# Tile 6 last in the last batch, and a recurrence that adds onto inputs kept in PSUM

## The chip, the cores and the metric

The kernel runs on one core of a Trainium2 chip. A core has five engines that run side by side, each in its own order: PE (matrix products, with a separate unit that loads weights, called PEld in the profile), ACT (functions such as exp, tanh and sigmoid), DVE (vector arithmetic), POOL (vector arithmetic too, slower) and SP, which here only issues DMA transfers. PE writes to PSUM, a small memory of banks from which ACT and DVE read; everything else is in SBUF or, outside the core, in DRAM. The metric is the device time of one execution in microseconds (us). Everything is in fp32, and a product of two fp32 operands counts as two matmul instructions in the profile, a transpose as one.

## The reference

The input x has 8 batches of 64 x 16 positions (1024 tokens) with 128 channels. Layer 0 is a convolution-like attention with 8 heads, two nested softmaxes and a feed-forward part. Layer 1, with which the change has to do, is this, token by token:

```
t = tokens(x)                                        # 8 x 1024 x 128
Bn = ln_t(t)                                         # LayerNorm without weights
Wi = Bn @ W.T
scores[b,i,j] = sum_d v[d] * tanh(Wi[b,i,d] + Wi[b,j,d])
t = t + softmax(scores, axis=-1) @ Bn                # attention
Wx = ln_t(t) @ Wf.T
Wx = (Wx - mean) * rsqrt(var + 1e-5) * gamma + beta  # mean and var over all 8192 tokens
y[b,-1] = 0;  y[b,n] = sigmoid(Wx[b,n] + y[b,n-1] @ V.T)     # 1024 steps
out = t + y
```

The scores are symmetric in i and j, so only the blocks on and above the diagonal need the tanh. The mean and the variance are taken over all tokens, so no step of the recurrence can begin before the last batch's attention is done.

## The kernel before

Both layers run batch by batch, layer 0 of batch b+1 beside layer 1 of batch b. Their instructions are not written in order: each piece of work is added to a planner (`Plan`) with the engine or engines that may do it, an estimated cost, the keys that it reads and writes, and a due time. `plan.emit()` then lists them for all engines, always taking the piece that can start first by the estimates and, among those, the one that is due first. So a change to what is added can move other instructions. What follows `plan.emit()` (line 1509) is written out in order.

**Attention of one batch in layer 1** (`layer1`, line 1275). The 1024 tokens are eight tiles of 128 rows. Row tile `it` computes the score blocks `it` to 7 of its rows. A group of rows is added up on DVE, POOL or ACT (lines 1164, 1168 and 1174), put through tanh on ACT (L1222; where ACT added, addition and tanh are one instruction, L1164), and multiplied with v on PE into the PSUM tile `sa` (L1242). When a row tile's scores are all there, ACT writes their exponentials to `E` (L1338); POOL halves the diagonal block and DVE adds its transpose (L1344, L1348). In most batches two row tiles share a pass; in the first and the last batch the order is a list of its own, `((4,), (5, 7), (6,), (0,), (1,), (2,), (3,))`.

As soon as row tiles 0 to `it` are done, `attention` (line 1357) handles output rows `it`: it transposes the blocks of `E` to the right of the diagonal into `ET` (L855, L867), multiplies the eight blocks with `Bn` (`attend`, L1371, with a 129th column that gives the softmax's denominator), and `add_to_x` divides and adds to `X` (L1375, L1376). After tiles 3 and 7 the four tiles are stored to `parked`, normalised (`layer_norm`: statistics on DVE, L814 and L815; the power -0.5 on POOL, L818 and L819; L824), transposed (`bT`) and projected (`projected`, L1265). `keep_wx` takes the statistics of the projection for the batch-wide mean (L1400) and copies it (L1401), in the last batch straight to `wx`.

**The recurrence** (from line 1512). The statistics of all batches are put together (L1514 to L1521) to a scale and an offset per channel. The 1024 steps of each batch are cut into 32 chunks of 32 steps that run side by side; each chunk starts 16 steps early from nothing (`EARLY`), so there are 16 + 32 = 48 steps, on 8 x 32 = 256 columns, in two halves of four batches. The inputs of 32 steps are scaled by DVE to `ws` (L1540). A step of a half is:

```
nc.tensor.matmul(to, ident, ws[:, l, bs, 0 : NCH - skip], start=True, stop=k == 0)   # L1552
nc.tensor.matmul(to, vf_sb, prev[half][:, :, skip:], start=False, stop=True)         # L1554
nc.scalar.activation(y[:, :, skip:], to, AF.Sigmoid)                                 # L1556
nc.vector.tensor_copy(ys[:, bs, l % NT, :, l // NT], y)                              # L1561, not in the first 16
```

The identity matmul brings the input into PSUM, the second adds the last state times V. When all steps are done, the output follows: 16 tiles of 512 columns, each of four transposes (L1570), an addition of the parked `X`, loaded as `xr` (L1526), on DVE (L1572), and a DMA by turns on ACT's queue and SP's (L1574).

Of the kernel before, what the change touches and what calls it, by code (L numbers as in the profile page):

```python
# [9 lines left out]
F32 = mybir.dt.float32  # L10
AF = mybir.ActivationFunctionType
ALU = mybir.AluOpType
AX = mybir.AxisListType
PSUM = bass.MemoryType.PSUM

P = 128
# [617 lines left out]
def fast_path(ctx: ExitStack, tc: tile.TileContext, a: dict, fits):  # L634
# [25 lines left out]
    def tile_of(pool, name, shape):  # L660
        return pool.tile(shape, F32, tag=name, name=name)
# [139 lines left out]

    stats = ring("stat", 7, [P, 4, 9])

    def layer_norm(src, kr, dst, kw, k, pri, on="POOL", then=None):


        st = stats[k]
        ks = ("stat", k)
        bn, mv, rs = st[:, :, 0:6], st[:, :, 6:8], st[:, :, 8]
        kw = kw if isinstance(kw, list) else [kw]  # L810

        def statistics(_):
            for j in range(4):
                nc.vector.bn_stats(out=bn[:, j, :], in_=src()[:, j, :])  # L814
                nc.vector.bn_aggr(out=mv[:, j, :], in_=bn[:, j, :])  # L815

        def power(_):
            nc.gpsimd.tensor_tensor(rs, mv[:, :, 1], eps, ALU.add)  # L818
            nc.gpsimd.tensor_tensor(rs, rs, neg_half[:, :4], ALU.pow)  # L819

        def normalise(e):
            if e == "DVE":
                for j in range(4):
                    nc.vector.tensor_scalar(  # L824
                        dst[:, j, :], src()[:, j, :], mv[:, j, 0:1], rs[:, j : j + 1], ALU.subtract, ALU.mult
                    )
            else:
                shape = [P, 4, C]
                nc.gpsimd.tensor_tensor(dst, src(), mv[:, :, 0:1].to_broadcast(shape), ALU.subtract)
                nc.gpsimd.tensor_tensor(dst, dst, rs.unsqueeze(2).to_broadcast(shape), ALU.mult)  # L830

        add(("DVE", 1.9), statistics, r=[kr], w=[ks], pri=pri)
        add(("POOL", 1.5), power, r=[ks], w=[ks], pri=pri)
        add((on, 1.1 if on == "DVE" else 2.2), normalise, r=[kr, ks], w=kw, pri=pri, give=then)

# [439 lines left out]
    def layer1(b):  # L1275
# [21 lines left out]

        E_at = E_first
        fills = [("fill", False), ("fill", True)]
        order = ((4,), (5, 7), (6,), (0,), (1,), (2,), (3,)) if early else shared  # L1300
        done, attended = set(), set()
        past = 0
        for pair in order:
# [48 lines left out]
            for it in range(NT):  # L1352
                if it not in attended and done.issuperset(range(it + 1)):
                    attended.add(it)
                    attention(b, it, X, kX, B, kB, E_at, L1)

    def attention(b, it, X, kX, B, kB, E_at, L1):

        for j0 in range(it + 1, NT, 4):
            js = range(j0, min(j0 + 4, NT))  # L1360
            through_bank(
                transposes([E_sb[:, E_at[it] + j - it, :] for j in js]), 0.08 + 0.12 * len(js),
                [("E", it, j) for j in js],
                copy(ET[:, j0 - 1 : j0 - 1 + len(js), :]), ("DVE", 0.15 + 0.132 * len(js)), [],
                [("ET", j) for j in js], L1,
            )

        def attend(bank):
            for j in range(NT):
                lhsT = E_sb[:, E_at[j] + it - j, :] if j <= it else ET[:, j - 1, :]  # L1370
                nc.tensor.matmul(bank[:, : C + 1], lhsT, B[:, j, :], start=j == 0, stop=j == NT - 1)  # L1371

        def add_to_x(_, bank):
            den = stats[5][:, 0, 0:1]
            nc.vector.reciprocal(den, bank[:, C : C + 1])  # L1375
            nc.vector.scalar_tensor_tensor(X[:, it, :], bank[:, :C], den, X[:, it, :], ALU.mult, ALU.add)  # L1376

        kg = kX + (it // 4,)
        through_bank(
            attend, 2.0,  # L1380
            [("E", j, it) for j in range(it + 1)] + [("ET", j) for j in range(it + 1, NT)]
            + [kB + (qh,) for qh in range(2)],
            add_to_x, ("DVE", 0.55), [kg], [kg], L1,
        )
        if it % 4 != 3:
            return
        qh = it // 4
        Xg = X[:, 4 * qh : 4 * qh + 4, :]
        add(
            ("SP", 4.0), lambda _: nc.sync.dma_start(  # L1390
                out=parked[b][512 * qh : 512 * qh + 512, :].rearrange("(t p) c -> p t c", p=P), in_=Xg
            ),
            r=[kg], w=[("parked", b, qh)], pri=L1,
        )
        layer_norm(lambda: Xg, kg, B2, kB2, 4, L1, "DVE" if b == NB - 1 else "POOL")

        kept = wx[:, b, 512 * qh : 512 * qh + 512] if b == NB - 1 else bT

        def keep_wx(_, bank):
            nc.vector.bn_stats(out=wx_stats[:, b, qh, :], in_=bank)  # L1400
            nc.vector.tensor_copy(kept, bank)  # L1401

        kq = ("e", 1, 1) if b == NB - 1 else ("bT",)
        projected(B2, kB2, wf_sb, (keep_wx, ("DVE", 1.4)), kq, L1, bT, ("bT",))
        if b < NB - 1:
            add(
                ("SP", 4.0),
                lambda _: nc.sync.dma_start(out=parked_wx[b][:, 512 * qh : 512 * qh + 512], in_=bT),
                r=[kq], w=[("wx", b, qh)], pri=L1,
            )  # L1410
# [95 lines left out]
    fetch_wx()  # L1506
    with tc.manual_schedule():
        plan.emit()
    main.close()


    rn = ctx.enter_context(tc.tile_pool(name="rn", bufs=1))
    mv = rn.tile([P, 2], F32, tag="mvb", name="mvb")
    nc.vector.bn_aggr(out=mv, in_=wx_stats.rearrange("p b s k -> p (b s k)"))  # L1514
    sc = rn.tile([P, 1], F32, tag="scb", name="scb")
    nc.vector.tensor_scalar(sc, mv[:, 1:2], EPS, None, ALU.add)
    nc.gpsimd.tensor_tensor(sc, sc, neg_half[:, 0:1], ALU.pow)
    nc.vector.tensor_tensor(sc, sc, gamma_sb, ALU.mult)
    off = rn.tile([P, 1], F32, tag="offb", name="offb")
    nc.vector.tensor_tensor(off, mv[:, 0:1], sc, ALU.mult)  # L1520
    nc.vector.tensor_tensor(off, beta_sb, off, ALU.subtract)  # L1521


    xr = rn.tile([P, NB, NT, C], F32, tag="xr", name="xr")
    for b in range(NB):
        nc.sync.dma_start(out=xr[:, b], in_=parked[b].rearrange("(p t) c -> p t c", t=NT))  # L1526

    EARLY = 16
    HB = NB // 2
    ws = rn.tile([P, LCH, NB, NCH], F32, tag="ws", name="ws")
    ys = rn.tile([P, NB, NT, NCH, LCH // NT], F32, tag="ys", name="ys")
    steps = wx.rearrange("p b (c l) -> p l b c", l=LCH)
    order = [LCH - EARLY + k for k in range(EARLY)] + list(range(LCH))
    for l in order[:LCH]:
        nc.vector.tensor_scalar(ws[:, l], steps[:, l], sc, off, ALU.mult, ALU.add)  # L1540
    with tc.tile_pool(name="ps_w", bufs=2, space=PSUM) as ps_w, tc.tile_pool(
        name="ps_t", bufs=4, space=PSUM
    ) as ps_t:
        prev = [None, None]
        for k, l in enumerate(order):
            early = k < EARLY
            skip = 1 if early else 0
            for half in range(2):
                bs = slice(half * HB, (half + 1) * HB)
                acc = ps_w.tile([P, HB, NCH], F32, tag=f"acc{half}", name=f"acc{half}")  # L1550
                to = acc[:, :, skip:]
                nc.tensor.matmul(to, ident, ws[:, l, bs, 0 : NCH - skip], start=True, stop=k == 0)  # L1552
                if k:
                    nc.tensor.matmul(to, vf_sb, prev[half][:, :, skip:], start=False, stop=True)  # L1554
                y = rn.tile([P, HB, NCH], F32, tag=f"y{half}", name=f"y{half}", bufs=3)
                nc.scalar.activation(y[:, :, skip:], to, AF.Sigmoid)  # L1556
                if k == EARLY - 1:

                    nc.vector.memset(y[:, :, 0:1], 0.0)
                if not early:  # L1560
                    nc.vector.tensor_copy(ys[:, bs, l % NT, :, l // NT], y)  # L1561
                prev[half] = y

        n = 0
        for b in range(NB):
            for g in range(2):
                pt = ps_t.tile([P, 4, C], F32, tag="yt", name="yt")
                for i in range(4):
                    t = 4 * g + i
                    nc.tensor.transpose(pt[:, i, :], ys[:, b, t].rearrange("p c j -> p (c j)"), ident)  # L1570
                ot = rn.tile([P, 4, C], F32, tag="ot", name="ot", bufs=4)
                nc.vector.tensor_tensor(ot, pt, xr[:, b, 4 * g : 4 * g + 4, :], ALU.add)  # L1572
                eng = nc.sync if n % 2 else nc.scalar
                eng.dma_start(  # L1574
                    out=a["out"][b].rearrange("(p t) c -> p t c", t=NT)[:, 4 * g : 4 * g + 4, :], in_=ot
                )
                n += 1


# [65 lines left out]
```

## Time and profile before

| | us |
|---|---|
| median of three runs | 5300.66 |
| their lowest and highest | 5299.17, 5303.35 |
| the profiled execution | 5300.69 |
| its span, first to last instruction | 5298.8 |
| ACT busy in the span | 4957.7 (94%) |
| PE busy | 4915.6 (93%) |
| DVE busy | 4739.3 (89%) |
| POOL busy | 4437.4 (84%) |

All lines of the profile are of that one execution. Times count from the span's start. A line of the timeline gives start, duration, engine, source line, operation, what is written and read with partitions x elements, the number of instructions put together, and in brackets how long the engine had been idle before and what released it. The granted clock is TensorE's, as a share of full speed; its mean over the span was 0.987.

The last batch's tanh work ends at 5206, the recurrence's first sigmoid starts at 5237.42 and its last at 5280.39, and the span ends at 5298.8.

### The profile page before, as it was taken

How to read it: one execution, taken by the hardware profiler on the slowest of the kernel's cores; microseconds unless marked ns; L12 is line 12 of the kernel's file. 1: busy time of each engine (PE TensorE's matmuls, PEld its weight loads, DVE VectorE, ACT ScalarE, POOL GpSimd, SP SyncE). 2: the span in 40 equal slices, each digit the busy share in tenths (PEclk: the TensorE clock that was granted, in tenths of full speed). 3: DMA queues.
4: the chain of work that ended last, by engine and by line, in shares of the span. 5: the costliest groups of instructions: out<-in, count | busy, mean ns of one | idle time of the engine just before them, and what ended most of it. 6: DMA issues, size and time to landing. Idle time of an engine off the chain costs nothing.

```text
span 5298.8 us, 184474 instructions
## 1 busy us (share of the span) xinstructions
PE 4915.6 (93%) x82181; PEld 3021.0 (57%) x82181; DVE 4739.3 (89%) x9090; ACT 4957.7 (94%) x3692; POOL 4437.4 (84%) x3064
## 2 busy tenths in 40 slices
PE   8899999999999999999999999999998999986567
PEld 6666656656665566556655566555664556552125
DVE  5788988889999999989998999989998999999886
ACT  4389999999999999999999999999999999999995
POOL 2366988679999899979999899989998989897992
PEclk9999999999999999999999999999999999998999
DMA  2000000000000000000000000000000000000001
GB/s 64 2 3 7 3 2 6 2 10 3 2 6 8 4 3 6 4 8 2 3 6 6 6 3 2 6 8 4 3 3 2 10 2 2 2 29 9 1 1 69
DMA packets 27669, 43.16 MB, mean 8 GB/s; under 512 B 2512, under 2 KB 19280, under 8 KB 26864
## 3 DMA queue, kind: packets, MB, share of 16 engines
q1 hardware_dynamic: 24832, 27.99, 1.6%
q8 instruction: 645, 10.57, 0.9%
q10 hardware_dynamic: 1872, 3.16, 0.2%
q14 instruction: 160, 1.31, 0.1%
q0 software_dynamic: 160, 0.13, 0.0%
HBM read 19.22 MB, written 12.06 MB: 6 GB/s over the span
## 4 chain that ended last, share of the span: by engine, by line
PE 67%; ACT 15%; DVE 11%; issue 5%; POOL 1%; DMA 0%; SPq 0%; ACTq 0%; DVEq 0%; POOLq 0%
PE sa L1242 23%; PE sc L948 14%; PE m L1050 13%; ACT th L1222 10%; DVE th L1168 3%; PE m L965 3%; ACT th L1164 3%; PE m L923 2%; PE m L982 2%; PE m L1371 2%; DVE stat_e L1027 2%; PE m L909 1%; DVE wx L990 1%; DVE th L1174 1%; PE m L1120 1%
## 5 line engine op out<-in xcount | busy, mean ns | idle before, releaser
L1174 POOL TENSOR_TENSOR th<-wiT 128x1024 f32<-128x1024 f32 (+55 forms) x2254 | 3255.7, 1479 | 308.9 <-PE sa L1242 270.3
L1222 ACT ACTIVATE th<-th 128x3210 f32<-128x3210 f32 (+57 forms) x1074 | 2926.5, 2767 | 27.0 <-DVE th L1174 15.6
L1242 PE MATMUL sa<-th,vpat 128*32 128x512 f32 (+33 forms) x24576 | 2045.9, 460 | 243.4 <-ACT th L1222 222.9
L1168 DVE TENSOR_SCALAR_CACHE_REDUCE th<-wiT 128x344 f32<-128x344 f32 (+61 forms) x2362 | 1945.8, 863 | 79.6 <-PE sa L1242 76.3
L1242 PEld LDWEIGHTS sa<-th,vpat 128*32 128x32 f32 x24576 | 715.7, 110 | 1186.2 <-issue 681.7
L1164 ACT ACTIVATE th<-wiT 128x501 f32<-128x501 f32 (+59 forms) x1544 | 1120.2, 797 | 16.1 <-PE sa L1242 14.9
L948 PE MATMUL sc<-xT,wx 128*32 128x256 f32 x16384 | 980.3, 380 | 2.2 <-issue 2.2
L1039 POOL TENSOR_TENSOR wx<-wx,stat_e 128x1024 f32<-128x1024 f32 x342 | 658.6, 1948 | 242.5 <-DVE stat_e L1030 153.9
L948 PEld LDWEIGHTS sc<-xT,wx 128*32 128x32 f32 x16384 | 549.9, 110 | 291.4 <-issue 45.5
L1050 PE MATMUL m<-wx 128*128 128x256 f32 x2400 | 563.1, 388 | 18.6 <-DVE stat_e L970 7.7
L1050 PEld LDWEIGHTS m<-wx 128*128 128x128 f32 x2400 | 449.6, 192 | 146.2 <-issue 45.6
L990 DVE TENSOR_TENSOR wx<-wx,m 128x1024 f32<-128x1024 f32 x330 | 396.9, 1206 | 38.6 <-PE m L982 36.8
L956 ACT ACTIVATE wx<-sc 128x1024 f32<-128x1024 f32 x342 | 340.3, 1022 | 93.8 <-PE sa L1050 35.9
L1042 DVE STREAM_TRANSPOSE wx<-wx 128x1024 f32<-128x1024 f32 x342 | 417.6, 1230 | 4.1 <-POOL wx L1039 3.6
L1039 POOL TENSOR_TENSOR e<-e,stat_e 128x1024 f32<-128x1024 f32 x170 | 327.1, 1946 | 97.6 <-DVE stat_e L1030 62.4
L1027 DVE TENSOR_REDUCE stat_e<-wx 128x128 f32<-128x2048 f32 x171 | 388.5, 2272 | 17.3 <-ACT wx L1024 16.1
L1024 ACT ACTIVATE wx<-wx 128x2048 f32<-128x2048 f32 x171 | 327.3, 1915 | 30.3 <-DVE wx L990 30.0
L982 PEld LDWEIGHTS m<-stat_e,ident 128*32 128x32 f32 x15808 | 224.0, 111 | 149.9 <-issue 76.7
L1050 PE MATMUL m<-e,wx 128*128 128x256 f32 x1184 | 278.6, 389 | 16.8 <-DVE e L1042 9.8
L1050 PEld LDWEIGHTS m<-e,wx 128*128 128x128 f32 x1184 | 221.7, 192 | 79.4 <-issue 21.7
L982 PE MATMUL m<-stat_e,ident 128*32 128x16 f32 x15808 | 229.2, 185 | 18.7 <-DVE stat_e L977 5.8
L1030 DVE RECIPROCAL stat_e<-stat_e 128x128 f32<-128x128 f32 x256 | 240.0, 938 | 0.2
(215 smaller groups left out, 4801.4 us busy)
## 6 DMA issues: line engine op xcount, KB each, us to landing
xT<-in_xt_dram SPq DMA_DIRECT2D x8, 512.0 KB, 3.4
th<-in_x_dram SPq DMA_DIRECT2D x8, 512.0 KB, 7.1
parked<-X SPq DMA_DIRECT2D x16, 256.0 KB, 2.3
xr<-parked SPq DMA_DIRECT2D x8, 512.0 KB, 6.9
parked_wx<-bT SPq DMA_DIRECT2D x14, 256.0 KB, 2.3
wx<-parked_wx SPq DMA_DIRECT2D x7, 512.0 KB, 3.7
out_dram<-ot ACTq DMA_DIRECT2D x8, 256.0 KB, 2.2
out_dram<-ot SPq DMA_DIRECT2D x8, 256.0 KB, 2.2
```

The costliest lines, as they stand in the source:

```text
L948: nc.tensor.matmul(sc[32 * a : 32 * a + 32, 256 * s : 256 * s + 256], u[:, rows], tokens[:, a], start=True, stop=True,)
L982: nc.tensor.matmul(bank[32 * a : 32 * a + 32, s * G : s * G + G], ident[:, 32 * s : 32 * s + 32], r1, start=True, stop=True,)
L990: nc.vector.tensor_tensor(quarters(e), quarters(e), r, ALU.mult)
L1027: nc.vector.tensor_reduce(r2, e2.rearrange("p q (m g) -> p q m g", g=G), AX.X, ALU.add)
L1039: nc.gpsimd.tensor_tensor(e3, e3, r2[:, q, :].unsqueeze(2).to_broadcast([P, M, G]), ALU.mult)
L1042: add(("DVE", 1.17), lambda _, e=e: nc.vector.transpose(e, e), r=[ke], w=[ke], pri=L0)
L1050: nc.tensor.matmul(bank()[:, :256], vp[:, t, :], keys[:, t], start=t == 0, stop=t == NT - 1)
L1164: nc.scalar.activation(rows(c)[:, r, :], wiT[:, i0 + begin[c] :], AF.Tanh, bias=w_i(c, r))
L1168: nc.vector.tensor_scalar(rows(c)[:, r, :], wiT[:, i0 + begin[c] :], w_i(c, r), 0.0, ALU.add, ALU.add, accum_out=next_unused())
L1174: eng.tensor_tensor(rows(c), wiT[:, i0 + begin[c] :].unsqueeze(1).to_broadcast(shape), w_i(c).unsqueeze(2).to_broadcast(shape), ALU.add,)
L1222: nc.scalar.activation(slot()[:, a:z], slot()[:, a:z], AF.Tanh)
L1242: nc.tensor.matmul(sa[32 * c : 32 * c + 32, s:s1], vpat[:, 31 - r0 - r : 63 - r0 - r], rows(c)[:, r, s - at0 - begin[c] : s1 - at0 - begin ...
```

## The change

1. In the last batch alone, row tile 6 moves from the third place of the order to the last one.
2. There, output rows 6 and 7 are not attended in one go: products that do not need tile 6's scores are summed ahead in a PSUM tile of their own (`scs[0]`, `scs[1]`), and the late ones (three) are added to them. The row tiles 4 to 7 take their LayerNorm statistics one by one.
3. The copy of the last half of `wx` is put behind the first three operations on the batch-wide statistics in the source, and a sigmoid of one column is written ahead of them.
4. The recurrence's inputs are no longer brought to PSUM by an identity matmul in each step. Four PSUM banks (two halves, four steps each, twofold) are written once by identity matmuls of 512 columns; after that DVE writes the scaled inputs of four steps and a half at a time straight into them, and V's matmul adds onto what is there (`start=False`). ACT writes its results directly to `ys` in the last 32 steps.
5. The output's layout on the chip has rows that belong to the first and the second half of each chunk's steps, and `xr` is loaded in 16 pieces of 256 KB instead of 8 of 512 KB. The 8 output tiles of the first half are made from step 32 of 48 on, two transposes a step, beside the remaining steps; the other 8 follow after the last step.

```
-        order = ((4,), (5, 7), (6,), (0,), (1,), (2,), (3,)) if early else shared
+        order = ((4,), (5, 7), (0,), (1,), (2,), (3,), (6,)) if b else ((4,), (5, 7), (6,), (0,), (1,), (2,), (3,))
+        order = order if early else shared
...
+        keys = {j: ("E", j, it) if j <= it else ("ET", j) for j in range(NT)}
+        ends = b == NB - 1 and it >= NT - 2
+        if ends:
+            at, kp = scs[it % 2][:, : C + 1], ("sc", it % 2)
+            late = [j for j in range(NT) if min(j, it) == NT - 2]
+            for js in ([j for j in range(NT) if j not in late], late):
+
+                def some(_, js=js):
+                    for j in js:
+                        lhsT = E_sb[:, E_at[j] + it - j, :] if j <= it else ET[:, j - 1, :]
+                        nc.tensor.matmul(at, lhsT, B[:, j, :], start=j == 0, stop=j == late[-1])
+
+                add(("PE", 0.22 * len(js)), some, r=[keys[j] for j in js] + [kB + (qh,) for qh in range(2)], w=[kp], pri=L1)
+            add(("DVE", 0.55), lambda _: add_to_x(_, at), r=[kp, kg], w=[kg], pri=L1)
...
+        if b == NB - 1 and it // 4 == 1:
+            bn, mv = stats[4][:, it % 4, 0:6], stats[4][:, it % 4, 6:8]
+
+            def statistics(_):
+                nc.vector.bn_stats(out=bn, in_=X[:, it, :])
+                nc.vector.bn_aggr(out=mv, in_=bn)
+
+            add(("DVE", 0.42), statistics, r=[kg], w=[("stat", 4)], pri=L1)
...
-            nc.vector.tensor_copy(kept, bank)
+            if b == NB - 1 and qh == 1:
+                last_half.append((kept, bank))
+            else:
+                nc.vector.tensor_copy(kept, bank)
...
+    nc.scalar.activation(off, eps[:, 0:1], AF.Sigmoid)
     nc.vector.bn_aggr(out=mv, in_=wx_stats.rearrange("p b s k -> p (b s k)"))
     nc.vector.tensor_scalar(sc, mv[:, 1:2], EPS, None, ALU.add)
     nc.gpsimd.tensor_tensor(sc, sc, neg_half[:, 0:1], ALU.pow)
+    for kept, bank in last_half:
+        nc.vector.tensor_copy(kept, bank)
...
+    for h in range(2):
+        for b in range(NB):
+            nc.sync.dma_start(out=xr[:, b, h].rearrange("p r k -> p (r k)"), in_=pieces(parked[b], h))
...
-    for l in order[:LCH]:
-        nc.vector.tensor_scalar(ws[:, l], steps[:, l], sc, off, ALU.mult, ALU.add)
...
+        ws = [[tile_of(ps_w, f"ws{half}{i}", [P, 4, HB, NCH]) for i in range(2)] for half in range(2)]
+        for i in range(2):
+            for half in range(2):
+                nc.tensor.matmul(
+                    ws[half][i].rearrange("p l b c -> p l (b c)"), ident, ident.unsqueeze(1).to_broadcast([P, 4, P]),
+                    start=True, stop=True,
+                )
+
+        def inputs(k):
+            skip = 1 if k < EARLY else 0
+            for l in (slice(0, 1), slice(1, 4)) if k == 0 else (slice(0, 4),):
+                for half in range(2):
+                    nc.vector.tensor_scalar(
+                        ws[half][k // 4 % 2][:, l, :, skip:],
+                        steps[:, order[k] + l.start : order[k] + l.stop, half * HB : half * HB + HB, 0 : NCH - skip],
+                        sc, off, ALU.mult, ALU.add,
+                    )
+
+        def tile_out(b, h):
+            pt = ps_t.tile([P, 4, C], F32, tag="yt", name="yt")
+            for r in range(4):
+                nc.tensor.transpose(pt[:, r, :], ys[:, b, h, r].rearrange("p i c -> p (i c)"), ident)
+                if r % 2:
+                    yield
+            ot = rn.tile([P, 4, C], F32, tag="ot", name="ot", bufs=4)
+            nc.vector.tensor_tensor(ot, pt, xr[:, b, h], ALU.add)
+            eng = nc.sync if b % 2 else nc.scalar
+            eng.dma_start(out=pieces(a["out"][b], h), in_=ot.rearrange("p r k -> p (r k)"))
...
-                nc.tensor.matmul(to, ident, ws[:, l, bs, 0 : NCH - skip], start=True, stop=k == 0)
+                to = ws[half][k // 4 % 2][:, k % 4, :, skip:]
                 if k:
-                    nc.tensor.matmul(to, vf_sb, prev[half][:, :, skip:], start=False, stop=True)
-                y = rn.tile([P, HB, NCH], F32, tag=f"y{half}", name=f"y{half}", bufs=3)
+                    nc.tensor.matmul(to, vf_sb, prev[half][:, :, skip:], start=False, stop=True, skip_group_check=True)
+                if early:
+                    y = rn.tile([P, HB, NCH], F32, tag=f"y{half}", name=f"y{half}", bufs=3)
+                else:
+                    y = ys[:, bs, l // HL, l % 4, l % HL // 4, :]
                 nc.scalar.activation(y[:, :, skip:], to, AF.Sigmoid)
...
-                if not early:
-                    nc.vector.tensor_copy(ys[:, bs, l % NT, :, l // NT], y)
...
+            if k % 4 == 3 and k + 5 < len(order):
+                inputs(k + 5)
+            if k >= EARLY + HL:
+                next(first_half, None)
+        for _ in first_half:
+            pass
+        for _ in outputs(1):
+            pass
```

## The prediction

> **What bounds the kernel now.** I read first a table of stretches (columns: us of the stretch, then PE, PEld, DVE, ACT, POOL busy us with counts, granted clock, DMA share, GB/s).
>
> ```profile
> 4600.00:4800.00 200.00, 180.12 (x2450) 99.51 (x2446) 183.37 (x487) 200.00 (x179) 182.75 (x135) 0.97 0.08 25
> 4880.00:5060.00 180.00, 105.22 (x972) 27.40 (x968) 147.97 (x280) 180.00 (x62) 167.47 (x106) 0.99 0.00 1
> 5210.00:5236.00 26.00, 15.80 (x100) 12.16 (x100) 15.14 (x52) 0.00 (x0) 2.99 (x5) 0.80 0.20 68
> 5240.00:5280.00 40.00, 40.00 (x361) 40.00 (x360) 26.30 (x84) 24.62 (x91) 0.00 (x0) 1.00 0.09 37
> 5280.00:5298.80 18.80, 9.17 (x68) 6.92 (x66) 10.94 (x19) 0.50 (x2) 0.00 (x0) 0.87 0.61 227
> ```
>
> ACT is busy without a gap until the last tanh; then it does nothing for 26 us, the close of the last batch. In 5240 to 5280, the recurrence, PE is busy all the time and ACT 24.6 of 40. The last 18.8 us are the output. So four stages, four limits: ACT; a serial chain; PE; DVE.
>
> The chain of work that ended last shows the close (start, us, what):
>
> ```profile
> 5206.25 1.13 PE sa L1242 x16
> 5207.40 0.71 ACT E L1338
> 5209.60 2.07 PE m L1371 x16
> 5212.30 2.07 PE m L1371 x16
> 5215.00 2.06 PE m L1371 x16
> 5219.43 3.59 PE m L1371 x32
> 5225.62 1.03 POOL stat L819
> 5229.10 2.09 PE m L1265 x2
> ```
>
> Tile 3's scores come last, and all row tiles from 3 on wait for them: five attends of 16 matmuls (L1371), statistics, two projections. Then lines of the timeline: the hinge, an early and a later step, and additions on DVE behind which ACT fell dry:
>
> ```profile
> 5231.22 0.70 DVE L1400 BATCH_NORM_STATS2 wx_stats<-m 128x6 f32<-128x512 f32 x1 [2.17 <-PE m L1265]
> 5231.83 0.67 DVE L1401 COPY wx<-m 128x512 f32<-128x512 f32 x1
> 5236.13 1.28 ACT L1556 ACT_TABLE_LOAD   x1 [28.03 <-DMA xr<-parked]
> 5238.58 0.27 ACT L1556 ACTIVATE y<-acc 128x124 f32<-128x124 f32 x1 [0.71 <-PE acc L1554]
> 5251.35 0.27 ACT L1556 ACTIVATE y<-acc 128x124 f32<-128x124 f32 x1 [0.17 <-PE acc L1554]
> 4842.91 17.87 DVE L1174 TENSOR_TENSOR th<-wiT 128x768 f32<-128x768 f32 x16 [0.38 <-PE sa L1242]
> 4860.81 2.10 ACT L1222 ACTIVATE th<-th 128x2280 f32<-128x2280 f32 x1 [2.19 <-DVE th L1174]
> 4512.94 10.81 DVE L1174 TENSOR_TENSOR th<-wiT 128x568 f32<-128x568 f32 x1
> ```
>
> Call S the start of the last statistics of wx, 5231.22.
>
> **The change part by part.** Sums go against the profiled run, 5300.69 (span 5298.8 and 1.9 around it), 0.03 over the median 5300.66.
>
> *Last batch, ACT's stretch (tile 6 moved from third to last).* Until about 4836 all queues issue what they issued. From there to the last tanh ACT does the same scores in other groups: summed at 0.833 ns an element plus 0.10 to 0.19 an instruction, 0.35 us less. The stall of 2.19 at 4860.81 stood behind additions before tile 6's scores, slowed to 17.87 us (10,656 elements; at 1.157 ns, by the 13.28 us for 11,472 at 4829.26, 12.3); the groups are cut anew, so I take it away. The last score matmuls are 32 of 128 columns instead of 16 of 388: 1.22 (the row at 4862.97) against 1.07. For new gaps I take 0.5, bounds 0 and 5: what the 7.2 us stall of the row at 4512 leaves at most of a lead that on DVE and POOL was 15 us at the end (their last additions end at 5192). Together -0.35 - 2.19 + 0.15 + 0.5 = -1.9 (-2.4 to +3).
>
> *The close.* Before, from the last score matmul's end (5207.32) to S: 23.9. After, the chain is: exponential 0.08 + 0.36 (128x256, at 4864.89), halving on POOL 0.08 + 0.46, transpose 0.33, addition on DVE 0.33, the late attend products 0.7 (of the sixteen of tiles 6 and 7 three come late, and thirteen are summed beforehand), twice reciprocal, X, statistics 1.85 (5223.04 to 5224.23 gives 0.54 for the first two and 0.4 for a pair of statistics), POOL 1.48, normalising to bT 1.68 (5226.68 to 5228.36), bT 0.74, projection with the clock still at 0.50 2.12. Sum 10.2, so -13.7 (bounds -12.5 and -15, the second with a warm projection: 1.12 at 5218.30). The attends of tiles 3 to 5 and the statistics and projection of tiles 0 to 3 now lie under ACT's stretch; what hides them there is that POOL was idle for 16.15 us before 5208.18 and PE busy 5.65 of the 10 us from 5200. Without that cover their 10.5 us (5208.85 to 5219.4) would come back.
>
> *Head of the recurrence.* The copy of wx, though deferred in the source, still stands between statistics and aggregate: no gain. New: four identity matmuls of 512 columns which prime PSUM banks, the first waiting for that copy (S+1.34). Cold each costs 2.08, warm 1.12, as L1265's. Writing of inputs waits for the first: S+3.47, where before the scale is ready too (5234.60 = S+3.38). Two pieces, then the table load 1.28, which the change means to move to the start: but in the issued order that sigmoid comes before the first exponential, and a load stays before the recurrence. First sigmoid S+5.8 (before S+6.20). Behind the four matmuls the first V matmul waits on PE: S+7.7 (S+9.7 if all stay cold). Before, the steady rhythm traced back from the last sigmoids (5279.94 less 46 steps) puts step 1's first sigmoid at S+7.64; after, S+7.7 + 0.47 = S+8.17. So +0.5 (0 to +2.5). The early sigmoid's extra table load at the start lies in the 1.30 us gap before the first exponential (30.60): 0, at most +1.3.
>
> *46 steps.* Before, a half step is 0.447 (5250.91 to 5251.35 to 5251.80), equal for 124 and 128 columns: four PE instructions, whose weight loads lie 0.112 apart. After, two of the four go, and the half's own chain is next: sigmoid 0.277, to PE 0.055, PE start to ACT start 0.47 (four transposes 5208.16 to the copy at 5208.85 is 0.69, less two of 0.112). 0.80 a step instead of 0.893: -4.3. Bounds 0.754 (weights ahead) and 0.893 (no gain): -6.4 to 0. The 64 copies of ys on DVE were beside PE: 0.
>
> *Half of the output beside the last steps.* New on PE: 32 transposes, by turns before a V matmul (0.112 to 0.22 each time); on ACT's queue four DMA issues of 0.34; each waits for an `ot` that DVE makes behind two writes of inputs (0.69 each), and the sigmoids behind it wait too. Two bunches of transposes at 0.5, four issues at 0.34 partly in ACT's 0.25 a step of idle, one wait of about 0.9: +2 (0.5 to 4).
>
> Recurrence: +0.5 - 4.3 + 2 = -1.8.
>
> *Output.* Eight of sixteen `ot` remain: 8 x 0.692 (2.60 to 2.69 for four, less waits as before) = -5.5, and of the 1.16 us in which they wait for DMAs some 0.2: -5.7 (-4.5 to -6.5). Loads of xr (16 of 256 KB, 4 MB in 12 us at some 400 GB/s) end well before the first `ot`: 0.
>
> **Sum:** -1.9 - 13.7 - 1.8 - 5.7 = -23.1: 5277.6.
>
> **The rivals.**
> 1. *The recurrence stays as long* (step 0.89: the path through ACT, PSUM and PE costs more than the transposes' row says). For it: the first cold step took 0.83 from V matmul to sigmoid. Then +4.3: 5282; with stalls at their upper bound 5284.
> 2. *The clock stays at 0.50* since PE is then busy only half the time. Rows: it rose 4.2 us after PE's return at 5235.3, with PE busy without gaps. Cold, PE start to ACT start is 0.83 (5237.75 to 5238.58), a step 1.16: 46 x 0.36 = +16.6, 5294.2: no change that can be measured (a measurement tells about 0.2%, 10.6 us). Against: 4880 to 5060 holds 0.99 with PE busy 105 of 180.
> [...]
> 3. *Slower:* tile 6's additions, last now, hold ACT up. DVE has 24 of them (20,188 elements, 23.4 us) ahead of ACT's last groups. One like 4512.94 costs 10.1 us over its 0.7, while POOL ran additions back to back. To end above 5311.3 ACT must lose 33 us on top of a lead of 15: five such hold-ups in the last tile. Four give 5277.6 + 40.4 - 15 = 5303, five 5313. Against: there was one of this size among the rows I read, and POOL was idle at this place.
>
> [...]
>
> **How the numbers follow.** Forecast 0.55, rival 1 0.25, rival 2 0.08, rival 3 0.05, and 0.07 for a loss in ACT's stretch or the close that I have not listed, half of it under the bound of 0.2%. Faster 0.87, same 0.08, slower 0.05. The bounds of the terms, taken as independent, give the forecast 5270 to 5286; with rival 1, and the edge of the unlisted, 5268 to 5289 leaves out about 0.2.
>
> **What the profile would show.** Right: some 17 us instead of 31.2 from the last tanh's end (5206.2) to the first sigmoid; S near 5215.6; a sigmoid every 0.40 us; 39 us from step 1's first sigmoid to the last, instead of 41.8; eight `ot` after it and 12.7 us to the end instead of 18.4. Wrong: PE's clock at 0.5 past S+12; ACT waiting for L1174 in the last 60 us; sigmoids that wait for a DMA issue; steps still 0.89 apart.

## The result: 0.3% slower

Over 16 runs each, the changed kernel has a median of 5317.26 us (5305.64 to 5323.26) and the kernel before 5300.26 (5290.00 to 5304.87). The ratio is 1.0034, with a 95% interval of 1.0027 to 1.0042: slower by some 18 us. The forecast was 5277.6, in a range of 5268 to 5289, with 0.05 on slower. It was wrong in its sign.

The profiled execution of the changed kernel took 5319.27 (span 5317.3), 18.6 more than that of the kernel before. Of this, 5.0 lie where both programs issue the same instructions in the same order: the first instruction of ACT that differs starts at 4835.11 before and at 4840.15 after. Why is not known; the last section shows how far that point lies apart between profiles. So from here on stages are counted from that instruction, in each profile, called the fork. S is, as in the prediction, the start of the last statistics of wx. All times in us; each entry is the difference of two starts or ends of the timeline.

| stage | before | predicted | after |
|---|---|---|---|
| fork to the end of the last tanh | 371.1 | 369.0 | 368.8 |
| to the end of the last score matmul | 1.1 | 1.3 | 4.2 |
| to S | 23.9 | 10.2 | 10.6 |
| S to the last sigmoid's end | 49.5 | 47.7 | 64.4 |
| to the end of the span | 18.1 | 12.4 | 29.1 |
| sum | 463.7 | 440.6 | 477.2 |

The close is as short as forecast. The loss is in the recurrence and the output. Three stretches from the table of stretches of the changed kernel (us, busy us of PE, PEld, DVE, ACT, POOL with counts, granted clock, DMA share, GB/s):

```profile
5228.00:5256.00 28.00, 24.04 (x124) 16.61 (x122) 19.11 (x21) 16.04 (x60) 0.00 (x0) 0.95 0.26 102
5256.00:5288.00 32.00, 18.29 (x111) 14.91 (x110) 12.17 (x15) 9.56 (x38) 0.00 (x0) 0.73 0.26 95
5290.00:5314.00 24.00, 1.56 (x11) 0.85 (x9) 4.15 (x6) 0.00 (x0) 0.00 (x0) 0.62 0.26 91
```

And the kernel before, while it loaded xr and while it stored the output:

```profile
5234.00:5242.00 8.00, 6.29 (x39) 6.04 (x39) 7.88 (x21) 3.67 (x11) 0.00 (x0) 0.66 0.99 393
5283.00:5296.00 13.00, 6.17 (x40) 3.96 (x38) 8.26 (x13) 0.00 (x0) 0.00 (x0) 0.93 0.84 310
```

In the changed kernel the DMA share is 0.26 in all three, at 91 to 102 GB/s: no engine is busy all the time, and the DMA engines are on average a quarter busy. Such an even quarter is what 4 of 16 engines working all the time would look like. Before, it was 0.99 and 393 GB/s during the loads and 0.84 and 310 GB/s during the output. The waits from S to the end (engine, line, waited for: us in total, times, longest):

```profile
DVE ot L1597 <- DMA out_dram<-ot: 25.2, 8, 7.4
ACT ys L1621 <- DVE ot L1597: 15.9, 3, 8.3
```

`ot` waits for one of its four buffers, whose transfer is not through; ACT's next sigmoid waits behind the DMA issue on its queue, which waits for `ot`. On the timeline:

```profile
5228.94 1.28 ACT L1621 ACT_TABLE_LOAD   x1 [15.32 <-DMA xr<-parked]
5231.89 0.27 ACT L1621 ACTIVATE y<-ws 128x124 f32<-128x124 f32 x1 [1.10 <-PE ws L1616]
5244.62 0.50 ACT L1621 ACTIVATE ys<-ws 128x128 f32<-128x128 f32 x2 [0.35 <-PE ws L1616]
5245.48 0.50 ACT L1621 ACTIVATE ys<-ws 128x128 f32<-128x128 f32 x2 [0.35 <-PE ws L1616]
5270.26 0.69 DVE L1597 TENSOR_TENSOR ot<-yt,xr 128x512 f32<-128x512 f32 x1 [5.33 <-DMA out_dram<-ot]
5270.98 0.55 ACTq L1599 DMA_DIRECT2D out_dram<-ot  x1
5271.57 0.45 ACT L1621 ACTIVATE ys<-ws 128x128 f32<-128x128 f32 x2 [6.47 <-DVE ot L1597]
5278.39 1.29 DVE L1597 TENSOR_TENSOR ot<-yt,xr 128x512 f32<-128x512 f32 x2 [7.44 <-DMA out_dram<-ot]
5280.30 0.45 ACT L1621 ACTIVATE ys<-ws 128x128 f32<-128x128 f32 x2 [8.28 <-DVE ot L1597]
5305.87 0.69 DVE L1597 TENSOR_TENSOR ot<-yt,xr 128x512 f32<-128x512 f32 x1 [3.69 <-DMA out_dram<-ot]
```

Steps run at 0.86 (5244.62 to 5245.48) until the output begins. Then ACT stands for 6.47 and 8.28: the issue at 5270.98 waits for the `ot` before it, and the sigmoid at 5271.57 for the issue. From 5269 to 5285 PE is busy 5.6 of 16 us; its granted clock is 0.50 there (1.00 from 5232 to 5268), and a step takes 1.16 (sigmoids at 5281.47 and 5282.63). After the last step five of the eight remaining `ot` wait for transfers again, 12.1 in all.

The chain of work that ended last shows the close, and what is new in it:

```profile
5208.32 1.79 PE m L1375 x16
5210.11 0.86 PE m L1266 x2
5210.97 2.25 PE sa L1243 x50
5213.24 0.39 ACT E L1340
5218.18 1.02 POOL stat L819
5221.66 2.09 PE m L1266 x2
5225.21 6.43 PE ws L1575 x8
```

The last score matmuls (L1243) stand on PE behind the attend of tile 5 and the projection of tiles 0 to 3; so 4.2 pass from the last tanh to their end, not 1.1.

### The profile page after: what moved, and what is told of

Its sections match the earlier page's. It is cut to its first block, busy times and chain, and to the rows that moved or that the text cites. A ratio compares the mean times of both kernels' runs of the same rounds, so it can differ in the third digit from the quotient of the medians.

```text
span 5317.3 us, 184017 instructions
## 1 busy us (share of the span) xinstructions
PE 4917.1 (92%) x81997; PEld 3010.9 (57%) x81997; DVE 4731.8 (89%) x9022; ACT 4957.7 (93%) x3691; POOL 4444.7 (84%) x3069
## 4 chain that ended last, share of the span: by engine, by line
PE 67%; ACT 15%; DVE 10%; issue 5%; POOL 1%; DMA 1%; ACTq 0%; SPq 0%; DVEq 0%; POOLq 0%
PE sa L1243 23%; PE sc L949 14%; PE m L1051 13%; ACT th L1223 10%; PE m L966 3%; DVE th L1169 3%; ACT th L1165 3%; PE m L924 2%; PE m L983 2%; PE m L1375 2%; DVE stat_e L1028 2%; PE m L910 2%; DVE wx L991 1%; PE m L1121 1%; PE m L856 1%
## 5 line engine op out<-in xcount | busy, mean ns | idle before, releaser
L1223 ACT ACTIVATE th<-th 128x3210 f32<-128x3210 f32 (+56 forms) x1075 | 2928.8, 2765 | 24.9 <-DVE th L1175 17.8
L1243 PE MATMUL sa<-th,vpat 128*32 128x512 f32 (+34 forms) x24576 | 2045.1, 460 | 233.8 <-ACT th L1223 212.0
L1243 PEld LDWEIGHTS sa<-th,vpat 128*32 128x32 f32 x24576 | 715.2, 110 | 1173.1 <-issue 682.2
L1025 ACT ACTIVATE wx<-wx 128x2048 f32<-128x2048 f32 x171 | 326.9, 1912 | 31.6 <-DVE wx L991 31.3
```

The costliest lines, as they stand in the source:

```text
L1223: nc.scalar.activation(slot()[:, a:z], slot()[:, a:z], AF.Tanh)
L1243: nc.tensor.matmul(sa[32 * c : 32 * c + 32, s:s1], vpat[:, 31 - r0 - r : 63 - r0 - r], rows(c)[:, r, s - at0 - begin[c] : s1 - at0 - begin ...
```

## The experiments

Theory A: loads of xr and stores of the output run on 4 of the 16 DMA engines, because their outermost dimension has four entries: the new layout reads and writes DRAM as 4 pieces x 32 chunks x 2 KB, the old one as 128 rows, of 4 KB in the loads and of 2 KB in the output. Theory B: DMA issues between the sigmoids and the sharing of queues are the cause. Each ratio is to the kernel before, run beside it on the same chip; its medians lie between 5291 and 5305 us on the five chips that were used, so a median is read against its own neighbour.

**Chunks outermost (e1).** The partitions are ordered chunk by piece instead of piece by chunk, and `ys` with them; so the sigmoids write with a step of four elements.

```
-        return tokens.rearrange("(c h i r) k -> h i c (r k)", h=2, i=4, r=4)[h]
+        return tokens.rearrange("(c h i r) k -> h c i (r k)", h=2, i=4, r=4)[h]
...
-    ys = rn.tile([P, NB, 2, 4, 4, NCH], F32, tag="ys", name="ys")
+    ys = rn.tile([P, NB, 2, 4, NCH, 4], F32, tag="ys", name="ys")
...
-                nc.tensor.transpose(pt[:, r, :], ys[:, b, h, r].rearrange("p i c -> p (i c)"), ident)
+                nc.tensor.transpose(pt[:, r, :], ys[:, b, h, r].rearrange("p c i -> p (c i)"), ident)
...
-                    y = ys[:, bs, l // HL, l % 4, l % HL // 4, :]
+                    y = ys[:, bs, l // HL, l % 4, :, l % HL // 4]
```

> The changed kernel with one thing different: in the transfers of xr and of the output the 32 chunks, not the 4 pieces of a chunk, are the outermost dimension on the DRAM side, and ys is laid out to match. Bytes, packet size (2 KB) and all waits stay. Theory A (a transfer whose outermost dimension has four entries is given to 4 of the 16 DMA engines: 102 GB/s and a DMA share of 0.25 in the changed kernel, where before had 400 GB/s): the share goes to near 1, xr lands within some 12 us, no ot waits over 1 us, ACT never waits for an ot over 2 us. Last sigmoid ends at S+50 (47 steps of 0.85 from S+8.1, and 2 of stalls), the end 13 later, S+63 instead of S+93.5: 31 us less than the changed kernel, about 5286. Theory B (DMA issues on ACT's queue between the sigmoids and the sharing of queues are the cause, whatever the layout): DMA share and time stay, 5312 to 5320.

Ratio to the kernel before 0.9989 (0.9980 to 0.9998), median 5294.90 against 5301.39. The loads, and a sigmoid in a late step:

```profile
5219.00:5229.00 10.00, 9.30 (x29) 4.88 (x28) 7.28 (x11) 4.32 (x13) 0.55 (x1) 0.75 0.96 337
5250.43 0.40 ACT L1621 ACTIVATE ys<-ws 128x128 f32<-128x128 f32 x1 [0.30 <-PE ws L1616]
```

The DMA share is 0.96, the table of waits from 5200 on has no `ot` that waits for a transfer, and last sigmoid to end is 13.1 instead of 29.1: theory A. The recurrence, 61.5, was expected at 50. The edit brought a cost of its own that I had not counted: with a step of four elements a sigmoid of 128 columns takes 0.40 instead of 0.28, and a step 1.19 (sigmoids at 5239.03 and 5240.22, at a clock of 1.00). From 5242 to 5258 the clock was 0.50 as well, and a step took 1.29 (5242.70 and 5243.99).

**Output left out of the step loop (e2).** The two lines `if k >= EARLY + HL: next(first_half, None)` are left out.

> The changed kernel, but no output tile is made beside the steps: all 16 follow after the last sigmoid; the layout of the transfers stays as in the changed kernel. Theory A (transfers at 102 GB/s are the limit from S on): xr takes 4.19 MB / 0.102 = 41 us from S+0.5, hidden by the steps; last sigmoid near S+48; then 16 output transfers of 2.57 us, 41 us: end near S+92, as in the changed kernel (S+93.5), so 5312 to 5319. Theory B (DMA issues between the sigmoids are the cause): the stalls go and the output takes 18.4 us as before: end near S+67, some 5291.

Ratio 1.0026 (1.0015 to 1.0037), median 5315.11. From S to the end 65.1 + 31.3. But the edit did not do what I meant: the framework that places instructions put eight `ot` between the steps all the same, with waits of up to 8.9 on ACT. So this is one more run of nearly the changed kernel, and it tells nothing between A and B.

**The layout alone in the kernel before (e3).**

```
-        nc.sync.dma_start(out=xr[:, b], in_=parked[b].rearrange("(p t) c -> p t c", t=NT))
+            nc.sync.dma_start(out=xr[:, b, h].rearrange("p r k -> p (r k)"), in_=pieces(parked[b], h))
...
-                    nc.vector.tensor_copy(ys[:, bs, l % NT, :, l // NT], y)
+                    nc.vector.tensor_copy(ys[:, bs, l // 16, l % 4, l % 16 // 4, :], y)
...
-                eng.dma_start(
-                    out=a["out"][b].rearrange("(p t) c -> p t c", t=NT)[:, 4 * g : 4 * g + 4, :], in_=ot
-                )
+                eng.dma_start(out=pieces(a["out"][b], g), in_=ot.rearrange("p r k -> p (r k)"))
```

> The kernel before, with only the changed kernel's layout of xr, ys and the output's transfers (16 loads, outermost dimension 4); recurrence, attention and the place of the output as before. Theory A: loads hidden behind the steps, but the 16 output transfers take 16 x 2.57 = 41 us and a landing after the first ot at 5281.5 instead of 17: about +25, 5325 (5318 to 5330). Theory B: no difference from before, 5298 to 5303.

Ratio 1.0068 (1.0052 to 1.0083), median 5331.69. Loads, then output:

```profile
5240.00:5265.00 25.00, 25.00 (x227) 25.00 (x226) 12.96 (x49) 15.46 (x57) 0.00 (x0) 1.00 0.27 102
5282.00:5324.00 42.00, 8.51 (x32) 5.86 (x32) 8.21 (x12) 0.00 (x0) 0.00 (x0) 0.54 0.26 99
```

Here no DMA is issued on ACT's queue between the sigmoids, and the recurrence takes 50.2 (49.5 before), but the output 49.6 instead of 18.1. The layout alone costs 31 us in the output, 6 more than expected: B can't explain that.

**Eight entries (e10).** The same kernel as e3 with partitions of 8 pieces of two steps x 16 chunks, so the rows are of 1 KB and there are twice as many transfers.

```
-        return tokens.rearrange("(c h i r) k -> h i c (r k)", h=2, i=4, r=4)[h]
+        return tokens.rearrange("(s c h i r) k -> s h i c (r k)", s=2, h=2, i=8, r=2)[s, h]
```

> The kernel before with a layout of xr and output whose outermost dimension has eight entries (8 x 16 rows of 1 KB, 128 KB a transfer, 32 loads and 32 output transfers) instead of four (e3) or 128. Theory A in the form: a transfer uses as many of the 16 DMA engines as its outermost dimension has entries: DMA share near 0.5 during the loads and, in the output, about twice the 102 GB/s of four entries, so 200 GB/s; 4.19 MB of output in 21 us, from the last sigmoid to the end 23 to 30 (18.1 before, 49.6 with four entries). If it is a threshold (anything under 16 goes to four engines): share 0.25, 49 us. If any outermost dimension over four is spread over all: share over 0.8, below 22 us.

One execution, 5313.64 against 5290.99 of the kernel before. Loads, then output:

```profile
5236.00:5250.00 14.00, 13.59 (x101) 13.30 (x101) 11.91 (x28) 7.71 (x28) 0.00 (x0) 0.82 0.53 185
5284.00:5308.00 24.00, 7.79 (x36) 5.62 (x34) 8.02 (x12) 0.00 (x0) 0.00 (x0) 0.60 0.53 170
```

Share 0.53; last sigmoid to end 30.8. So with 4, 8, 32 and 128 entries the share during the loads is 0.26, 0.53, 0.96 and 0.99. Of 16 engines, 4 and 8 at work all the time would be 0.25 and 0.5; with 32 and 128 entries nearly all were at work. The packets show it too: the trace has the start and the duration of each one. During the loads four packets of 2 KB are under way for 84% of the time in the changed kernel (5228 to 5256), seven to nine for over 85% in e10 (5236 to 5250), and 15 to 17, of 4 KB, for 85% in the kernel before (5234 to 5242). A packet of 2 KB has the same median of 84 ns in the changed kernel and in e1, so it is the number of engines at work that differs, and not their speed.

**The attention half of the change alone (e4).** All of the changed kernel up to the planner's end, with recurrence and output of the kernel before.

> Only the first half of the change: tile 6 last, attends of tiles 6 and 7 summed ahead, statistics one by one; recurrence and output as before. From the trace of the changed kernel: ACT's stretch -2.3, the last score matmuls on PE +3.1, from their end to S 10.6 instead of 23.9 (-13.3): together -12.5, 5288 (5284 to 5292). If the common part of the program, which is 5 us longer in the changed kernel's profile without a change in it, is longer because of something in this half, then 5293; if the order's gain is an artefact of the one profile, 5300.

Ratio 0.9977 (0.9968 to 0.9987), median 5288.35 against 5301.39. From the fork 452.4 instead of 463.7: 368.7, 4.2, 10.6, 50.5, 18.4. By the stages this half brings 11 us, by the medians 13, as expected; some 2 us of it are not the order's, as the account of the prediction below shows.

**Four transfers for each tile (e5).** The changed kernel's own `ys`, each tile moved in four pieces of 32 chunks.

```
-            nc.sync.dma_start(out=xr[:, b, h].rearrange("p r k -> p (r k)"), in_=pieces(parked[b], h))
+            for i in range(4):
+                nc.sync.dma_start(
+                    out=xr[32 * i : 32 * i + 32, b, h].rearrange("p r k -> p (r k)"), in_=pieces(parked[b], h)[i]
+                )
...
-            eng = nc.sync if b % 2 else nc.scalar
-            eng.dma_start(out=pieces(a["out"][b], h), in_=ot.rearrange("p r k -> p (r k)"))
+            eng = nc.sync if b % 2 or h == 0 else nc.scalar
+            for i in range(4):
+                eng.dma_start(
+                    out=pieces(a["out"][b], h)[i], in_=ot[32 * i : 32 * i + 32].rearrange("p r k -> p (r k)")
+                )
```

> The changed kernel with its own layout of ys (contiguous writes of the sigmoids), but each load of xr and each output tile is cut into four transfers of 64 KB, one for each of the 4 pieces, so that the outermost dimension has 32 entries; the first half's are all issued on SP's queue. Theory A (4 of 16 DMA engines): DMA share near 1 during the loads, no ot waits for a transfer over 2 us, steps of 0.85 without stalls over 1 us; from S the last sigmoid ends at +50 and the end at +64 instead of +93.5: 30 us under the changed kernel, 5286 (5282 to 5291), and 9 under the version with the strided ys, whose sigmoids take 0.40 instead of 0.28. If DMA issues on ACT's queue or the sharing of queues had been the greater part, transfers of 64 KB would bring less than 10 us against the changed kernel.

Ratio 0.9987 (0.9978 to 0.9996), median 5291.44 against 5300.41: the gain on the changed kernel is there, though 5 less than expected. From S to the last sigmoid 47.3, better than expected; the output 21.0, worse. The DMA issues from S on (issue, KB each, median us to landing):

```profile
xr<-parked SPq DMA_DIRECT2D x64, 64.0 KB, 2.0
out_dram<-ot SPq DMA_DIRECT2D x48, 64.0 KB, 1.8
out_dram<-ot ACTq DMA_DIRECT2D x16, 64.0 KB, 2.6
```

The medians to landing are under 3 us, but while xr is loaded (5210 to 5232) they bring 135 GB/s at a DMA share of 0.43: 65.5 KB in 0.48 us, one issue of SP after the other. Issuing now looks like the limit; e8 tries that.

**The same with the output out of the step loop (e7).** As in e2, and with SP and ACT by turns.

> As the kernel with four transfers, but all 16 output tiles after the last sigmoid. It prices the half output beside the steps: if that costs the steps nothing, the last sigmoid ends at the same S+50 and the output takes 18.4 as before instead of 13.1: +5. If the transposes, the DMA waits and DVE's ot hold up the steps by the 2 us that the prediction took, S+48 and then 18.4: +3.

Ratio 1.0003 (0.9994 to 1.0012), median 5302.08. Again output was placed between the steps (six `ot` before the last sigmoid), now with issues on ACT's queue: 49.2 and 30.4. It does not price what it was meant to.

**Pairs of batches in a transfer (e8).**

```
+                two_out = a["out"][b - 1 : b + 1].rearrange("b (c h i r) k -> h i c b (r k)", h=2, i=4, r=4)[h]
+                for i in range(4):
+                    eng = nc.sync if i % 2 or h == 0 else nc.scalar
+                    eng.dma_start(out=two_out[i], in_=ot[32 * i : 32 * i + 32].rearrange("p b r k -> p b (r k)"))
```

> As the kernel with four transfers, but the output transfers of two batches are one (128 KB, outermost dimension 32, one for each of the 4 pieces), half as many, and those of the second half go by turns on both queues. In the run with four transfers each issue took 0.45 to 0.6 us, so that 64 KB at a time gave 142 GB/s and 21.0 from the last sigmoid to the end. If the number of issues is that limit: 13 to 15 from the last sigmoid to the end, steps unchanged (S to last sigmoid 47 to 49); measured from the point where the two programs part, 443 instead of 450.4 and of 463.7 in the kernel before. If something else limits the transfers (the 32 rows of each), it stays at 21.

Ratio 0.9966 (0.9952 to 0.9980), median 5273.03 against 5291.48. This version is 0.3% faster than the kernel before. From the fork 444.8, against 463.7 before: 368.5, 3.0, 10.6, 47.3, 15.5. With half as many issues in the output, 15.5 instead of 21.0 pass from the last sigmoid to the end. That is what fewer issues should bring, though less than the 13 to 15 expected; but the edit also keeps six output tiles on the chip instead of four, and DVE's waits for a free one went from 11.1 to 6.4 in all. Which of the two brought how much was not separated.

**All output behind the steps (e12).** The recurrence and the output of e8 in the order in which they are written (`tc.manual_schedule()`), 16 tiles after the last sigmoid.

> The kernel in pairs, with the recurrence and the output issued in the order in which they are written and all 16 output tiles behind the last sigmoid (in the two earlier runs meant for this, eight tiles were still placed between the steps). It prices the half output beside the steps. If it costs the steps nothing: S to the last sigmoid 47.3 as in pairs, and the output 16 tiles instead of 8, 5.5 to 8 longer than the 15.5 in pairs: 443 + 6 from the point where the programs part. If the transposes and ot hold up the steps by the 2 us of the prediction: 45.3 and +4. With nothing between the steps each takes 0.85, 46 of them 39.1.

Ratio 1.0002 (0.9993 to 1.0012), median 5304.41. From step 1's first sigmoid to the last one's end 39.75, in e8 39.86: the transposes, `ot` and their DMAs cost the steps 0.1, not the 2 of the prediction. The output takes 30.5 instead of 15.5, more than the 5.5 to 8 expected: 15 us is what half of it beside the steps is worth with transfers of this form, in this order of writing. S to the first sigmoid is also 1.6 longer here, by the order of the head.

**The head (e6).** On e5: the table load as a piece of the planner in the close, and the banks primed with products of bf16 zeros.

```
+            add(("ACT", 1.5), lambda _: nc.scalar.activation(off, eps[:, 0:1], AF.Sigmoid), r=[("stat", 4)], w=["off"], pri=L1)
...
-                    ws[half][i].rearrange("p l b c -> p l (b c)"), ident, ident.unsqueeze(1).to_broadcast([P, 4, P]),
+                    ws[half][i].rearrange("p l b c -> p l (b c)"), prime, prime.unsqueeze(1).to_broadcast([P, 4, P]),
```

> As the kernel with four transfers, and two things at the head of the recurrence: the sigmoid that loads the table is a piece of the planner behind the last LayerNorm statistics (so ACT loads it while it has nothing to do, and the one at the start is gone), and the PSUM banks are primed with products of zeros in bf16 instead of the fp32 identity. By the trace of the changed kernel the four priming products take 6.43 us (cold) from S+1.44, the table load 1.28 before the first sigmoid at S+6.46, and step 1's sigmoid comes at S+8.1. If both were on the path: first sigmoid at about S+4.2, step 1's at S+5.2, and with some colder steps the whole 2 to 3 us shorter than with four transfers alone. If the scale and offset were the path: no difference.

Ratio 1.0000 (0.9991 to 1.0009), median 5301.96: ten worse than e5. The first sigmoid came at S+5.3, earlier by 1.2, but S to the last took 55.8 instead of 47.3. PE's clock was 0.50 over the 29 us from 5233 to 5262, at 1.16 a step.

**bf16 priming alone (e11).** On e8.

> The kernel in pairs with one thing different: the PSUM banks are primed by products of zeros in bf16 instead of the fp32 identity. If the clock of PE follows from the priming (6.4 us of it in fp32, at S+1.4 to S+7.9, after which the clock was 1.00): the clock stays at 0.50 until the transposes of the output begin, a step takes 1.16 for at least the first 25 steps, and S to the last sigmoid is 55 instead of 47.3, as in the run of the head. If it was the earlier table load or chance: 46 to 48.

One execution, 5298.08 (the kernel before beside it 5290.99); S to the last sigmoid 57.2. The clock, in e11 and then in e8, where the fp32 products prime:

```profile
5232.00:5262.00 30.00, 30.00 (x105) 24.04 (x105) 13.51 (x15) 14.23 (x53) 0.00 (x0) 0.50 0.35 106
```

```profile
5215.00:5240.00 25.00, 21.30 (x124) 15.85 (x124) 16.20 (x17) 14.69 (x59) 0.00 (x0) 1.00 0.41 130
```

It is the priming, the only difference between the two. With 6.4 us of fp32 products the clock was 1.00 and stayed there with the thin steps; after bf16 priming, which takes 1.9 us, the same steps did not raise it from 0.50 before the output's transposes came on top (from 5263.47 on). Whether the type of the products counts or only how long they take was not separated.

**PE kept at work in the close (e9).** On e8: the early table load of e6, fp32 priming, and three products of 512 columns, read by nobody, between the last attends and the last projection.

```
+                    nc.tensor.matmul(
+                        scs[0][:, 512:1024].rearrange("p (l c) -> p l c", c=P), ident,
+                        ident.unsqueeze(1).to_broadcast([P, 4, P]), start=True, stop=True,
+                    )
```

> As the kernel in pairs, with the table load moved into the close as in the run of the head, the priming in fp32 as in the changed kernel, and three products of 512 columns, whose results nobody reads, between the last attends and the last projection, where PE waits some 3.7 us. In the run of the head, with priming in bf16, PE's clock stayed at 0.50 for 35 us and a step took 1.16. Theory: PE's clock follows its work of the last few us; kept busy it stays at 1.00: the last projection takes 1.1 instead of 2.1, the four priming products 4.5 instead of 6.4, the first V matmul comes at S+6.0 instead of S+7.7; together with the projection 3 us less than in pairs. If the extra products come late, they hold up the last transposes and the gain is 1 or less. If the clock is not set by this, the durations stay and the extra products cost up to 3.

Ratio 0.9971 (0.9959 to 0.9982), median 5279.47 against 5291.48: no better than e8. The three products share a PSUM tile with the attends, and the next DVE instruction, the reciprocal, started after 3.38 of idle time, behind them: the close took 13.2. The last projection still took 2.08, and the priming 5.14 instead of 6.43 (4.5 expected); S to the last sigmoid is 46.8, in e8 47.3. Whether PE can be kept at full clock there, without such a wait, stays open.

## Why the prediction was wrong, step by step

- *Output, "Loads of xr (16 of 256 KB, 4 MB in 12 us at some 400 GB/s) end well before the first `ot`: 0"* and *"8 x 0.692"*: this is the step that failed. I took the rate of transfers from rows of transfers with another shape: 128 rows outermost. With four entries outermost both loads and stores ran at some 100 GB/s. The loads' 4.2 MB alone take 41 us at that rate, and the first `ot` started 36 us after S, at 5259.90. 8.4 MB at that rate are 82 us from S, and the kernel had 68 us from S to its end before. Measured: output +11.0 instead of -5.7, and in the recurrence two stalls of 6.47 and 8.28. Shown by e1, e3 and e10.
- *Half of the output beside the last steps, +2 (0.5 to 4):* some +16.6 in place of it, for the same reason: from step 1's first sigmoid to the last one's end 56.3, against 39.75 in e12 with no output between the steps. Of this, 15.9 are ACT's waits for `ot`. The wait "behind two writes of inputs" was the wrong wait; `ot` waits for a transfer, and ACT's queue hands it on to the recurrence. With the transfers mended it is 0.1 (e8, e12).
- *46 steps, 0.80:* 0.85. Sigmoid 0.27 and the way to PE 0.06 were right; PE start to ACT start took 0.52 and not 0.47 (5244.10 to 5244.62). That is about midway between the forecast and rival 1: of the 4.3 us, some 2 came.
- *Head:* step 1's first sigmoid at S+8.1, forecast S+8.17. The table load took 1.28 and the first sigmoid began 0.01 after it (5228.94, 5230.23).
- *The close, -13.7:* -13.3. Right in mechanism and size; e4 shows it alone.
- *ACT's stretch, -1.9 with the last score matmuls +0.15:* -2.3 for the stretch, but that agreement is luck. e3 and e10 keep the old order of row tiles and take 369.0 and 368.8 from the fork to the last tanh, as long as the changed kernel. The stall of 2.19 at 4860.81, which I took away for the new order, stands in neither of them: it belonged to the one profile before, and the order brought nothing here. And it took 4.2 instead of 1.3 to the end of the last score matmul. I had counted that PE had idle time enough for the moved attends, not where they would stand in its order.
- *Rival 2, the clock at 0.50:* not from the start; but behind the first stall the clock fell to 0.50 for some 16 us, and in e6 and e11 it stayed there from the start, each time at exactly the price given, 1.16 a step. What I did not see is what saves the changed kernel at first: its fp32 priming (6.43 us of it, and 1.00 from 5232 on). Having instructions under way did not by itself raise the clock: in e11 PE had them for all 30 us from 5232 to 5262 by the modelled ends, at 0.50.
- *Rival 3:* ACT did not wait for additions in the last 60 us.

My chances had no case for slow transfers at all: the layout of the output stood in the diff, and I had costed it at nothing.

## What to carry to other kernels

When an edit changes the layout of a tile, read every DMA that touches it as a new transfer: write down its outermost dimension on the DRAM side, and take its rate only from a row of the same shape. With 4, 8, 32 and 128 entries the DMA engines were busy to 0.26, 0.53, 0.96 and 0.99; cutting the tile into many small transfers gave only a part of the share back (0.43), with one issue every 0.48 us. And a wait on a queue that also carries a recurrence was paid there (6.47 and 8.28 us on ACT), however far behind the transfer seemed.

## What the runs showed of the hardware

In the profiles one addition on DVE takes either 10.8 us or 0.85, in a place that the change does not touch. In the changed kernel's profile, and then in e8's:

```profile
4517.92 10.79 DVE L1175 TENSOR_TENSOR th<-wiT 128x568 f32<-128x568 f32 x1
```

```profile
4513.44 0.85 DVE L1175 TENSOR_TENSOR th<-wiT 128x568 f32<-128x568 f32 x1
```

It is the row that rival 3 was built on. Of the 14 profiles, 11 show it at 10.8, each with ACT waiting some 7.2 behind it, and 3 (e2, e5, e8) at 0.85. In these three the fork lies at 4824 to 4829, in the others at 4833 to 4843. In the kernel before's profile POOL ran eight additions back to back beside it, for 9.99. But in e8's it ran as many back to back beside the short one, so that alone does not decide; there it was POOL's first addition that took longer, 1.65 instead of 1.13. And among the 11 the fork itself still lies up to 10 us apart. What decides between the two was not tried; a difference under some 10 us should be counted from the fork, or over many runs.

The second is the clock: the same thin load of PE that kept a clock of 1.00 (e8, 5215 to 5240) did not raise it from 0.50 (e11, 5232 to 5262).
